# A graph layer whose first part becomes a pipeline over three batches, with two weight rows per frequency instead of three

## The chip, the cores and the metric

The kernel runs on one core of a Trainium2 chip. The metric is the device time of one launch in microseconds (us). TensorE does the matrix products (PE in the profile, PEld for its weight loads), VectorE (DVE) and ScalarE (ACT) the elementwise work, GpSimd (POOL) a little arithmetic, and SyncE (SP) issues most transfers. Data lie in HBM, in the on-chip SBUF (128 partitions) and in PSUM (eight banks, where TensorE writes).

## The reference, cut to what matters

```python
def ref(x, adj, ...):                      # x (32, 512, 256), adj (32, 512, 512), fp32
    h = max(layernorm(x), 0)
    c = relu(bn1(conv1(h)))                # kernel of width 1, 256 -> 256 channels
    x_conv = relu(bn2(conv2(c)) + h)       # kernel of width 17, 256 -> 256, padding 8
    s = h @ w_se.T + b_se                  # 3 features per node
    A = exp(-dist(s, s)) * adj
    x_nmp = A @ relu(h @ w_msg.T + b_msg)
    gi = concat(x_conv, x_nmp) @ w_ih.T + b_ih
    gh = h @ w_hh.T + b_hh
    r, z = sigmoid(gi_r + gh_r), sigmoid(gi_z + gh_z)
    n = tanh(gi_n + r * gh_n)
    return x + (1 - z) * n + z * h
```

The convolution of width 17 is done in the frequency domain. Each sequence of 512 is cut into 8 windows of 64, each window is transformed at 80 points, so there are 40 units: unit 0 holds the two real frequencies, units 1 to 39 a complex frequency each. In each unit a complex product over 256 input channels is needed, and it is done with three real products instead of four.

## The kernel before, in words

The 32 batches are worked in two groups of 16. The program has five stages, one after the other on TensorE:

1. First part of group 0. For each batch: layer norm (`layer_norm`, L221: four statistics and four aggregates on VectorE, one power on GpSimd at L229, four normalisations at L232), eight transposes to channels-by-nodes (L243) that VectorE evicts with the ReLU (L244), a store of that tile to HBM (`hd`, L245), the convolution of width 1 (L256, VectorE adds the shift at L259, ScalarE the ReLU at L260), and the transform of the windows (L270, ScalarE copies at L273 into `xf`). Beside it the 17 taps of conv2 are transformed (`weights_to_freq`, L197): `load_taps` brings 8 input channels of each of four quarters (two transfers per quarter, of 16 taps and of the 17th), small products over 17 taps run four at a time on four row groups (L206), VectorE and ScalarE evict them by turns (L213, L215), and SyncE stores them to `wd` in HBM (L218). There are 64 such products of four, in 16 pieces, spread over the first 12 batches (`early = 12`).
2. Nodes of group 0 (messages L333, features, factors L353, distances L367, affinity, aggregation L381), with the 40 units of group 0 (`product`, L284) spread over the batches: `load_unit` loads the unit's three weight rows, GpSimd forms `both` = re + im (L294), TensorE does six matmuls (L299), ScalarE and VectorE evict `y` (L300, L304).
3. First part of group 1, without weights.
4. The rest of group 0: back transform (L411), gates (L421), output (L464 to L467), with the 40 units of group 1.
5. Nodes and rest of group 1.

The order within each engine is set by a scheduler that takes the instructions in program order as a priority and moves them where it expects an engine to be free. Tiles come from pools with a number of buffers: `x` has 2, `hT` 2, `wst` 6, `w2p` 2, `wt` 3, `both` 2. A load into a buffer waits for the last reader of the tile that had it. In stage 1 SyncE issues, in one queue: the loads of `x`, the stores `hd`, the tap loads and the stores `wd`.

For each frequency `wd` holds three rows, worked out by the transform of the taps: Wr, and two sums of Wr and Wi, so that the three products (re + im)·Wr, re·(second row) and im·(third row) give what the back transform needs; the sums are in the constants:

```python
    weights[:, 3::3], weights[:, 4::3], weights[:, 5::3] = cos, -sin - cos, cos - sin
```

Of the kernel before, what the change touches and what calls it, by code (L numbers as in the profile page):

```python
# [1 line left out]

# [12 lines left out]
P = 128  # L15
# [9 lines left out]
L = 80  # L25
UNITS = L // 2
ROWS = 3 * UNITS


def dft_constants(taps):  # L30
# [10 lines left out]
    weights = np.zeros((L, ROWS))  # L41
# [4 lines left out]
    back[3::3], back[4::3], back[5::3] = 2 * (cos - sin).T, -2 * sin.T, -2 * cos.T  # L46

    return [a.astype(np.float32) for a in (forward, weights[:taps][::-1], back / L)]
# [3 lines left out]
def gnn_layer(  # L52
# [38 lines left out]
    def load_x(b):  # L91
        X[b] = work.tile([P, NC, D], FP, tag="x", name=f"x_{b}", bufs=2)
        nc.sync.dma_start(X[b], x[b].rearrange("(c p) d -> p c d", p=P))


    load_x(0)
    ident = consts.tile([P, P], FP, name="ident")
# [12 lines left out]
    taps = consts.tile([P, ROWS], FP, name="taps")  # L110
    taps_dram = nc.inline_tensor(taps_np, name="dft_taps").ap()
    for q in range(4):
        nc.scalar.dma_start(taps[32 * q : 32 * q + 16, :], taps_dram[0:16, :])
        nc.scalar.dma_start(taps[32 * q + 16 : 32 * q + KT, :], taps_dram[16:KT, :])
    back = consts.tile([ROWS, L], FP, name="back")
    nc.scalar.dma_start(back, nc.inline_tensor(back_np, name="dft_back").ap())
# [25 lines left out]
    ones = consts.tile([P, P], FP, name="ones")  # L142
    nc.vector.memset(ones, 1.0)
    row1 = bank("row1")
    for i, v in enumerate((scale1, shift1)):
        for c in range(DC):
            diag = work.tile([P, P], FP, tag="diag", name=f"diag_{i}_{c}")
            nc.vector.tensor_scalar(diag, ident, v[:, c : c + 1], None, op0=ALU.mult)
            nc.tensor.matmul(row1[:, i * D + c * P : i * D + (c + 1) * P], ones, diag, start=True, stop=True)
# [11 lines left out]
    def load_weights():  # L161
        nc.scalar.dma_start(wmsg[:, :, :D], w_msgT.rearrange("(c p) o -> p c o", p=P))
        nc.scalar.dma_start(wmsg[:, :, D:], w_seT.rearrange("(c p) t -> p c t", p=P))
        nc.scalar.dma_start(bmsg[:, :D], b_msg.to_broadcast([P, D]))
        nc.scalar.dma_start(bmsg[:, D:], b_se.rearrange("t o -> o t").to_broadcast([P, NS]))
        nc.scalar.dma_start(whh, w_hhT.rearrange("(c p) o -> p c o", p=P))
        nc.scalar.dma_start(wih, w_ihT.rearrange("(c p) o -> p c o", p=P))
# [10 lines left out]
    WD = dram.tile([ROWS, D, D], FP, name="wd")  # L178
# [8 lines left out]
    W2P, WST = {}, {}  # L187

    def load_taps(gen, pc):
        t = W2P[pc] = gen.tile([P, PI, D], FP, tag="w2p", name=f"w2p_{pc}", bufs=2)  # L190
        for q in range(4):
            i0 = QI * q + PI * pc
            src = w2T[i0 : i0 + PI].rearrange("i k o -> k i o")
            nc.sync.dma_start(t[32 * q : 32 * q + 16], src[0:16])
            nc.sync.dma_start(t[32 * q + 16 : 32 * q + KT], src[16:KT])

    def weights_to_freq(gen, pc, part):  # L197
        per = N // D
        for q in range(4):
            WST[q] = gen.tile([ROWS, SI, D], FP, tag="wst", name=f"wst_{pc}_{part}_{q}", bufs=6)  # L200
        for s in range(0, SI, per):
            i = part * SI + s
            ps = []
            for q in range(4):
                p = bank(f"pw_{pc}_{i}_{q}")
                nc.tensor.matmul(p[:ROWS, :], taps[32 * q : 32 * q + KT, :],  # L206
                                 W2P[pc][32 * q : 32 * q + KT, i : i + per, :], start=True, stop=True)
                ps.append(p)
            for q in range(4):
                dst = WST[q][:, s : s + per, :]  # L210
                src = ps[q][:ROWS, :].rearrange("r (i d) -> r i d", d=D)
                if q % 2:
                    nc.vector.tensor_copy(dst, src)  # L213
                else:
                    nc.scalar.copy(dst, src)  # L215
        for q in range(4):
            i0 = QI * q + PI * pc + SI * part
            nc.sync.dma_start(WD[:, i0 : i0 + SI, :], WST[q])  # L218


    def layer_norm(b):  # L221
# [5 lines left out]
        rstd = work.tile([P, NC], FP, tag="rstd", name=f"rstd_{b}")  # L227
        nc.vector.tensor_scalar(rstd, mv[:, :, 1], LN_EPS, None, op0=ALU.add)
        nc.gpsimd.tensor_tensor(rstd, rstd, minus_half[:, :NC], op=ALU.pow)  # L229
        XN[b] = X[b]  # L230
# [48 lines left out]
    def load_unit(pw, g, u):  # L279
        t = WT[g, u] = pw.tile([P, DC, 3, D], FP, tag="wt", name=f"wt_{g}_{u}", bufs=3)  # L280
        for ic in range(DC):
            nc.sync.dma_start(t[:, ic], WD[3 * u : 3 * u + 3, ic * P : (ic + 1) * P, :].rearrange("k p o -> p k o"))

    def product(pw, g, u, xf):  # L284
        load_unit(pw, g, u)
        wt = WT.pop((g, u))
        re, im = xf[:, :, 2 * u, :], xf[:, :, 2 * u + 1, :]
# [193 lines left out]
    def first_part(g, xf, between):  # L481
        b0, b1 = g * GB, (g + 1) * GB
        if b0 not in X:
            load_x(b0)
# [3 lines left out]
        for b in range(b0, b1):  # L488
            if b + 1 < b1:
                layer_norm(b + 1)  # L490
# [159 lines left out]
```

## Time and profile before

| | |
|---|---|
| median of 3 runs | 2166.65 us (2163.05 to 2168.56) |
| the profiled execution's own time | 2165.15 us |
| its span, first to last instruction | 2163.3 us |
| mean granted TensorE clock | 0.972 |
| TensorE busy, share of the span | 96% |
| VectorE, ScalarE, GpSimd busy | 41%, 26%, 5% |
| moved by transfers | 308.89 MB |

Busy time of TensorE is the union of modelled matmul spans, so a stretch that reads 95% can still hold waits. A wait is best read in the lists of waits and in the chain, which is the work followed back from the last instruction: each piece stands with its start and the time it added. In tables by stretches the columns are: start:end and length, busy us (and count) of each engine, the granted TensorE clock, the busy share of the transfer engines, and GB/s. Group rows end with: count | busy us in total, mean ns of one | idle us of the engine just before them and what ended it. Rows that begin with SPq show how long SyncE's queue needed to issue a transfer, which includes the time that it was held up.

### The profile page before, as it was taken

To read this page: it belongs to the slowest core of one execution; us is meant where nothing else is said; L and a number is where in the kernel's file an instruction comes from. 1 tells how busy PE (TensorE), PEld (TensorE's weight loads), DVE (VectorE), ACT (ScalarE), POOL (GpSimd) and SP (SyncE) were. 2 spreads that over 40 slices of the span, in tenths; PEclk is the share of its full clock that TensorE was granted. 3 is DMA by queue.
4 is the path that set the end of the run, shared out by engine and by line. 5 is a ranking of instruction groups with operands and counts; after the bars stand their busy time and mean duration, and the time that the engine had idled before them with its cause. 6 is when DMAs were issued, how large, how long until landed. Compare 5 with 4: busy or idle time off the path is not lost.

```text
span 2163.3 us, 20486 instructions
## 1 busy us (share of the span) xinstructions
PE 2074.0 (96%) x7616; PEld 1258.4 (58%) x7616; DVE 887.8 (41%) x1893; ACT 557.5 (26%) x882; POOL 97.4 (5%) x119
## 2 busy tenths in 40 slices
PE   5878999999998999999999999999999999999998
PEld 3655766666687555555565555555555555555554
DVE  5555655545586222322232223433334444333343
ACT  1333423333234111111111111222223222222231
POOL 1000010001011000000000000000000000000000
PEclk7787999999999999999999999999999999999999
DMA  7777789889945444464345436232232333322210
GB/s 211 233 246 246 226 232 245 247 237 239 286 143 170 132 146 137 143 187 147 123 149 182 139 116 145 71 70 67 67 67 67 77 84 86 89 67 67 67 39 20
DMA packets 257922, 308.89 MB, mean 143 GB/s; under 512 B 12831, under 2 KB 224799, under 8 KB 257823
## 3 DMA queue, kind: packets, MB, share of 16 engines
q1 hardware_dynamic: 243840, 272.93, 45.8%
q10 hardware_dynamic: 13983, 34.65, 4.3%
q8 instruction: 60, 0.98, 0.2%
q14 instruction: 39, 0.32, 0.1%
HBM read 202.68 MB, written 104.86 MB: 142 GB/s over the span
## 4 chain that ended last, share of the span: by engine, by line
PE 86%; DVE 7%; DMA 3%; issue 2%; ACT 1%; POOL 1%; SPq 0%; ACTq 0%; DVEq 0%; POOLq 0%
PE pg L421 30%; PE pn L381 10%; PE pgi L421 10%; PE py L299 8%; PE pc L411 5%; PE pgh L421 5%; PE pc L256 4%; PE pm L333 4%; PE px L270 2%; DMA x<-in_x_dram 2%; PE pw L206 2%; PE pd L367 1%; PE po L464 1%; DVE at L372 1%; DVE stats L225 1%
## 5 line engine op out<-in xcount | busy, mean ns | idle before, releaser
L421 PE MATMUL pg<-nmp,wih 128*128 128x512 f32 x512 | 240.8, 592 | 0.0
L421 PE MATMUL pg<-hT,whh 128*128 128x512 f32 x512 | 240.6, 592 | 0.0
L421 PE MATMUL pg<-xconv,wih 128*128 128x512 f32 x512 | 240.6, 592 | 0.0
L436 ACT ACTIVATE rz<-pg,brz 128x512 f32<-128x512 f32 x128 | 87.9, 687 | 558.3 <-PE pg L421 558.3
L381 PE MATMUL pn<-A,msg 128*128 128x512 f32 x512 | 227.2, 597 | 1.5 <-DVE A L373 1.5
L447 DVE SCALAR_TENSOR_TENSOR n<-pgh,vec,rz 128x512 f32<-128x512 f32 x64 | 47.8, 747 | 399.9 <-PE pgh L421 399.9
L304 DVE COPY y<-py 128x256 f32<-128x256 f32 x78 | 32.9, 423 | 395.9 <-PE py L299 395.9
L421 PEld LDWEIGHTS pg<-xconv,wih 128*128 128x128 f32 x512 | 97.3, 190 | 122.5 <-issue 122.5
L421 PEld LDWEIGHTS pg<-nmp,wih 128*128 128x128 f32 x512 | 97.2, 190 | 122.0 <-issue 121.7
L381 PEld LDWEIGHTS pn<-A,msg 128*128 128x128 f32 x512 | 98.0, 192 | 119.6 <-issue 114.4
L421 PEld LDWEIGHTS pg<-hT,whh 128*128 128x128 f32 x512 | 97.3, 191 | 108.3 <-issue 104.3
L299 PE MATMUL py<-wt,xf 128*128 128x256 f32 x640 | 153.2, 381 | 0.0
L372 DVE STREAM_TRANSPOSE at<-adj 128x512 f32<-128x512 f32 x128 | 134.4, 1084 | 13.5 <-DMA adj<-in_adj_dram 13.3
L256 PE MATMUL pc<-w,hT 128*128 128x256 f32 x512 | 134.5, 422 | 0.4 <-DVE hT L244 0.4
L333 PE MATMUL pm<-wmsg,hT 128*128 128x259 f32 x512 | 131.9, 412 | 0.0
L411 PEld LDWEIGHTS pc<-back,yt 120*128 120x128 f32 x1024 | 120.6, 193 | 18.4 <-issue 18.2
L449 ACT ACTIVATE n<-n,vec 128x512 f32<-128x512 f32 x64 | 46.2, 722 | 330.2 <-DVE n L448 330.2
L299 PEld LDWEIGHTS py<-wt,xf 128*128 128x128 f32 x640 | 121.6, 191 | 16.4
L333 PEld LDWEIGHTS pm<-wmsg,hT 128*128 128x128 f32 x512 | 123.3, 327 | 13.0 <-issue 6.8
L256 PEld LDWEIGHTS pc<-w,hT 128*128 128x128 f32 x512 | 107.5, 215 | 30.7 <-ACT wst L215 10.3
L411 PE MATMUL pc<-back,yt 120*128 120x80 f32 (+1 forms) x1024 | 119.2, 275 | 3.2 <-DMA yt<-yd 3.2
L421 PE MATMUL pgh<-hT,whh 128*128 128x512 f32 x256 | 121.9, 598 | 0.0
(82 smaller groups left out, 2312.3 us busy)
## 6 DMA issues: line engine op xcount, KB each, us to landing
wt<-wd SPq DMA_DIRECT2D x160, 384.0 KB
x<-in_x_dram SPq DMA_DIRECT2D x64, 512.0 KB
adj<-in_adj_dram SPq DMA_DIRECT2D x128, 256.0 KB
wd<-wst SPq DMA_DIRECT2D x64, 480.0 KB
yd<-y ACTq DMA_DIRECT2D x80, 384.0 KB
yt<-yd SPq DMA_DIRECT2D x64, 480.0 KB
hT<-hd SPq DMA_DIRECT2D x48, 512.0 KB
hd<-hT SPq DMA_DIRECT2D x32, 512.0 KB
```

Of the source, the lines that this page charges most:

```text
L206: nc.tensor.matmul(p[:ROWS, :], taps[32 * q : 32 * q + KT, :], W2P[pc][32 * q : 32 * q + KT, i : i + per, :], start=True, stop=True)
L256: nc.tensor.matmul(p[:, j, :], HT[b][:, ic, c * P : (c + 1) * P], w1[:, ic, :], start=(ic == 0), stop=(ic == DC - 1))
L270: nc.tensor.matmul(p[:, j * 2 * L : (j + 1) * 2 * L], H1[b][:, c0 + j, ic * P : (ic + 1) * P], fwd, start=True, stop=True)
L299: nc.tensor.matmul(dst, v[:, ic, :], wt[:, ic, k, :], start=(ic == 0), stop=(ic == DC - 1))
L333: nc.tensor.matmul(p[:, : D + NS], chunk(HT[b][:, ic, :], c), wmsg[:, ic, :], start=(ic == 0), stop=(ic == DC - 1))
L372: nc.vector.transpose(at.rearrange("p (j k) -> p j k", k=32), ADJ[b].rearrange("p j (q c) -> p c j q", c=NC)[:, mc])
L381: nc.tensor.matmul(p, MSG[b][:, mc, dc * P : (dc + 1) * P], A[b][:, mc, :], start=(mc == 0), stop=(mc == NC - 1))
L411: nc.tensor.matmul(p[:, t0:t1], YT[b][w][:, oc * P : (oc + 1) * P], back[:, u0 : u0 + t1 - t0], start=(w == 0), stop=(w == W - 1), skip_gr ...
L421: nc.tensor.matmul(p, w, v, start=(i == 0), stop=(i == len(terms) - 1))
L436: nc.scalar.activation(RZ[b][:, g, :], p, AF.Sigmoid, bias=brz[:, g : g + 1], scale=1.0)
L447: nc.vector.scalar_tensor_tensor(n, ph, b_hn[:, i : i + 1], RZ[b][:, i, :], op0=ALU.add, op1=ALU.mult)
L449: nc.scalar.activation(n, n, AF.Tanh, bias=b_in[:, i : i + 1], scale=1.0)
```

## The change

It has three parts.

The rows. `wd` holds Wr and Wi only (`WROWS` = 80 instead of 120), so a store of `wst` has 320 KB instead of 480 KB and `load_unit` loads 256 KB per unit in two transfers instead of 384 KB. `product` lets GpSimd form three tiles per unit: re + im, im − re (128x256 each), and `wsum` = Wr + Wi (128x512, new). The products are (im − re)·Wr, (re + im)·Wi and re·wsum, in this order; `wsum` is thus read last. The back transform's constants are adapted. The number and shape of the matmuls stay.

The first part, in both groups. `layer_norm` is split into `statistics` and `normalise`. In a step for batch b, three batches are in work: statistics and normalisation of b + 2, transposes of b + 1, convolution of b, and transform of the windows of b − 1. `x` gets 3 buffers, `wst` 8, and its loads from batch b0 + 3 on, as well as the tap loads after the first two, are issued by GpSimd's queue instead of SyncE's. The weight products are spread over all 16 batches, two products of four per batch, one before and one behind the windows; of eight evictions VectorE does three (before four). The block stands under `tc.manual_schedule()`, which keeps the program's order on each engine. `wih` and the other weights of the later stages are loaded at batch 8 by SyncE (before: at the start, by ScalarE's queue).

In the stage of the nodes two units, not one, stand before `factors` of the next batch. The taps' constants are laid out for four quarters and come in one transfer, not eight.

```diff
-    weights[:, 3::3], weights[:, 4::3], weights[:, 5::3] = cos, -sin - cos, cos - sin
+    weights[:, 2::2], weights[:, 3::2] = cos, -sin
...
-    def load_x(b):
-        X[b] = work.tile([P, NC, D], FP, tag="x", name=f"x_{b}", bufs=2)
-        nc.sync.dma_start(X[b], x[b].rearrange("(c p) d -> p c d", p=P))
+    def load_x(b, queue=nc.sync):
+        X[b] = work.tile([P, NC, D], FP, tag="x", name=f"x_{b}", bufs=3)
+        queue.dma_start(X[b], x[b].rearrange("(c p) d -> p c d", p=P))
...
-    WD = dram.tile([ROWS, D, D], FP, name="wd")
+    WD = dram.tile([WROWS, D, D], FP, name="wd")
...
-    def load_taps(gen, pc):
+    def load_taps(gen, pc, queue=nc.gpsimd):
...
+            queue.dma_start(t[32 * q : 32 * q + 16], src[0:16])
+            queue.dma_start(t[32 * q + 16 : 32 * q + KT], src[16:KT])
...
-                if q % 2:
-                    nc.vector.tensor_copy(dst, src)
+            if q == 3 or (q == 1 and s == 0):
+                nc.vector.tensor_copy(dst, src)
...
     def load_unit(pw, g, u):
-        t = WT[g, u] = pw.tile([P, DC, 3, D], FP, tag="wt", name=f"wt_{g}_{u}", bufs=3)
-        for ic in range(DC):
-            nc.sync.dma_start(t[:, ic], WD[3 * u : 3 * u + 3, ic * P : (ic + 1) * P, :].rearrange("k p o -> p k o"))
+        t = WT[g, u] = pw.tile([P, 2, DC, D], FP, tag="wt", name=f"wt_{g}_{u}", bufs=3)
+        for k in range(2):
+            nc.sync.dma_start(t[:, k], WD[2 * u + k].rearrange("(i p) o -> p i o", p=P))
...
-            both = pw.tile([P, DC, P], FP, tag="both", name=f"both_{g}_{u}", bufs=2)
-            nc.gpsimd.tensor_tensor(both, re, im, op=ALU.add)
+            both = pw.tile([P, 2, DC, P], FP, tag="both", name=f"both_{g}_{u}", bufs=2)
+            nc.gpsimd.tensor_tensor(both[:, 0], re, im, op=ALU.add)
+            nc.gpsimd.tensor_tensor(both[:, 1], im, re, op=ALU.subtract)
+            wsum = pw.tile([P, DC, D], FP, tag="wsum", name=f"wsum_{g}_{u}", bufs=2)
+            nc.gpsimd.tensor_tensor(wsum, wr, wi, op=ALU.add)
             p2 = bank(f"py2_{g}_{u}")
-            terms = [(p[:, :D], both), (p[:, D : 2 * D], re), (p2[:, :D], im)]
+            terms = [(p2[:, :D], both[:, 1], wr), (p[:, D : 2 * D], both[:, 0], wi), (p[:, :D], re, wsum)]
...
         for b in range(b0, b1):
-            if b + 1 < b1:
-                layer_norm(b + 1)
-            if b + 2 < b1:
-                load_x(b + 2)
-            between(b - b0)
-            conv1(b)
+            one, two = between(b - b0)
+            if b + 3 < b1:
+                load_x(b + 3, nc.gpsimd)
+            if b + 2 < b1:
+                statistics(b + 2)
             if b + 1 < b1:
                 transpose_h(b + 1)
-            windows_to_freq(b, xf)
+            if b + 2 < b1:
+                normalise(b + 2)
+            conv1(b)
+            for step in one:
+                step()
+            if b > b0:
+                windows_to_freq(b - 1, xf)
+            for step in two:
+                step()
+        windows_to_freq(b1 - 1, xf)
...
-                    for u in mine[:1]:
+                    for u in mine[:2]:
                         product(pw, 0, u, xf)
                     if more:
                         factors(b + 1)
-                    for u in mine[1:2]:
-                        product(pw, 0, u, xf)
                     aggregate(b)
```

Three places show how instructions move. The first is TensorE in the first part of group 0. `pc` is the convolution, `phT` a transpose, `px` the transform of the windows, `pw` a weight product. Before, at batch 2 (h_2 goes into px in the step in which it is made):

```order
L256 MATMUL pc_2_0_549<-w_77,hT_420 128x256 x4
L256 MATMUL pc_2_2_556<-w_77,hT_420 128x256 x4
L243 MATMUL phT_0_564<-ident,x_362 128x128 x4
L243 MATMUL phT_1_570<-ident,x_362 128x128 x4
L270 MATMUL px_0_0_577<-fwd,h_2_548 128x160 x2
L270 MATMUL px_0_2_581<-fwd,h_2_548 128x160 x2
L270 MATMUL px_1_0_585<-fwd,h_2_548 128x160 x2
L270 MATMUL px_1_2_589<-fwd,h_2_548 128x160 x2
L206 MATMUL pw_0_0_616<-w2p_396,taps 120x512
L206 MATMUL pw_0_1_618<-w2p_396,taps 120x512
```

Now, the step of batch 2:

```order
L257 MATMUL phT_0_467<-ident,x_266 128x128 x4
L257 MATMUL phT_1_473<-ident,x_266 128x128 x4
L270 MATMUL pc_2_0_485<-w_79,hT_361 128x256 x4
L270 MATMUL pc_2_2_492<-w_79,hT_361 128x256 x4
L213 MATMUL pw_0_0_503<-w2p_204,taps 80x512
L213 MATMUL pw_0_1_505<-w2p_204,taps 80x512
L213 MATMUL pw_0_2_507<-w2p_204,taps 80x512
L213 MATMUL pw_0_3_509<-w2p_204,taps 80x512
L284 MATMUL px_0_0_515<-fwd,h_1_379 128x160 x2
L284 MATMUL px_0_2_519<-fwd,h_1_379 128x160 x2
L284 MATMUL px_1_0_523<-fwd,h_1_379 128x160 x2
L284 MATMUL px_1_2_527<-fwd,h_1_379 128x160 x2
```

The transposes (of batch 3) went ahead of the convolution of batch 2, four weight products stand between, and the windows transformed are those of batch 1, made a step earlier.

The second place is GpSimd's queue in the first part of group 0. `rstd` is the power of the layer norm, in the order of the batches. Before, the powers stand alone:

```order
L229 TENSOR_TENSOR rstd_226<-rstd_226,minus_half 128x4
L229 TENSOR_TENSOR rstd_259<-rstd_259,minus_half 128x4
L229 TENSOR_TENSOR rstd_355<-rstd_355,minus_half 128x4
L229 TENSOR_TENSOR rstd_460<-rstd_460,minus_half 128x4
L229 TENSOR_TENSOR rstd_603<-rstd_603,minus_half 128x4
```

Now, from the power of batch 2 on (the pair of tap loads stands four times):

```order
L240 TENSOR_TENSOR rstd_278<-rstd_278,minus_half 128x4
L99 DMA x_346<-in_x_dram 128x4x256
L240 TENSOR_TENSOR rstd_358<-rstd_358,minus_half 128x4
L200 DMA w2p_442<-in_w2T_dram 16x8x256
L201 DMA w2p_442<-in_w2T_dram 1x8x256
...
L99 DMA x_451<-in_x_dram 128x4x256
L240 TENSOR_TENSOR rstd_463<-rstd_463,minus_half 128x4
L99 DMA x_547<-in_x_dram 128x4x256
```

Between the power of batch 3 (`rstd_358`) and that of batch 4 (`rstd_463`) stand now eight tap loads, which wait for the last product that reads the old `w2p`, and a load of `x`. That is so at every second batch, six times in all.

The third place is TensorE in the nodes of group 0, around `factors` (psl and psr). `py` is a unit, `pn` the aggregation. Before:

```order
L299 MATMUL py_5_2203<-wt_5_2199,both_5_2204 128x256 x2
L299 MATMUL py_5_2203<-wt_5_2199,xf_215 128x256 x2
L299 MATMUL py_0_5_2206<-wt_5_2199,xf_215 128x256 x2
L353 MATMUL psl_2216<-ident,fl 128x128 x4
L353 MATMUL psr_2223<-ident,fr 128x128 x4
L299 MATMUL py_6_2234<-wt_6_2230,both_6_2235 128x256 x2
L299 MATMUL py_6_2234<-wt_6_2230,xf_215 128x256 x2
L299 MATMUL py_0_6_2237<-wt_6_2230,xf_215 128x256 x2
L381 MATMUL pn_0_2248<-A_2134,msg_2026 128x512 x4
```

Now:

```order
L317 MATMUL py_0_5_2224<-wt_5_2214,both_5_2219 128x256 x2
L317 MATMUL py_5_2218<-wt_5_2214,both_5_2219 128x256 x2
L317 MATMUL py_5_2218<-wsum_5_2222,xf_213 128x256 x2
L317 MATMUL py_0_6_2244<-wt_6_2234,both_6_2239 128x256 x2
L317 MATMUL py_6_2238<-wt_6_2234,both_6_2239 128x256 x2
L317 MATMUL py_6_2238<-wsum_6_2242,xf_213 128x256 x2
L371 MATMUL psl_2254<-ident,fl 128x128 x4
L371 MATMUL psr_2261<-ident,fr 128x128 x4
L399 MATMUL pn_0_2269<-A_2149,msg_2032 128x512 x4
```

`psl` and `psr` moved behind the second unit, and the last pair of each unit now reads `wsum`.

More of the change, by code (lines that the diff above doesn't have):

```diff
@@ L193, in load_taps, with weights_to_freq @@
             src = w2T[i0 : i0 + PI].rearrange("i k o -> k i o")
-            nc.sync.dma_start(t[32 * q : 32 * q + 16], src[0:16])
-            nc.sync.dma_start(t[32 * q + 16 : 32 * q + KT], src[16:KT])
-    def weights_to_freq(gen, pc, part):
+            queue.dma_start(t[32 * q : 32 * q + 16], src[0:16])
+            queue.dma_start(t[32 * q + 16 : 32 * q + KT], src[16:KT])
+    def weights_to_freq(gen, pc, i):
         per = N // D
-        for q in range(4):
[L200 to L203, printed above, removed]
-            for q in range(4):
[L205 to L211, printed above, removed]
-                if q % 2:
[L213 to L218, printed above, removed]
```

119 lines of the change are left out of this document (75 added, 44 removed).

## The prediction

> **What bounds the kernel now.** I read the page first, then a table by the program's stages, the chain of waits in the first part, and a timeline of one stretch there.
>
> ```profile
> span 2163.3 us, 20486 instructions
> PE 2074.0 (96%) x7616; PEld 1258.4 (58%) x7616; DVE 887.8 (41%) x1893; ACT 557.5 (26%) x882; POOL 97.4 (5%) x119
> PE 86%; DVE 7%; DMA 3%; issue 2%; ACT 1%; POOL 1%; SPq 0%; ACTq 0%; DVEq 0%; POOLq 0%
> ```
>
> TensorE holds 86% of the chain, so most of the program can't gain from anything but fewer or faster matmuls, and the change has just as many of the same shape. The question is where the other 14% lie. By stage (first part, nodes, first part of group 1, rest, last stage):
>
> ```profile
> 0.00:251.50 251.50, 200.69 (x905) 145.23 (x906) 138.32 (x359) 81.64 (x160) 18.22 (x25) 0.81 0.74 232
> 251.50:583.60 332.10, 317.67 (x1247) 218.11 (x1247) 181.22 (x432) 103.77 (x169) 34.71 (x41) 0.99 0.88 245
> 583.60:703.50 119.90, 108.84 (x641) 96.86 (x639) 84.64 (x247) 46.17 (x96) 15.50 (x16) 1.00 0.51 172
> 703.50:1395.00 691.50, 686.67 (x2314) 389.19 (x2315) 184.09 (x287) 121.23 (x178) 28.92 (x37) 0.99 0.48 140
> 1395.00:2163.30 768.30, 760.11 (x2516) 409.05 (x2514) 299.54 (x568) 204.69 (x279) 0.00 (x0) 1.00 0.28 67
> ```
>
> The first part is the only stage with large holes: TensorE is idle for 51 of 251.5 us, and its granted clock is 0.81. What its work would take without holes is read from the chain, where pieces stand back to back at full clock:
>
> ```profile
> 222.81 3.45 PE pc L256 x16
> 226.27 0.89 PE phT L243 x8
> 227.17 4.30 DMA x<-in_x_dram
> 242.10 0.55 PE px L270 x4
> 242.67 1.90 PE px L270 x12
> 251.56 2.90 PE pm L333 x12
> ```
>
> A batch needs 3.45 + 0.89 + 0.55 + 1.90 = 6.8 us, and the transposes of one batch are followed by 4.30 us of waiting for the `x` of a later one. The weight products and the engines around them, in a stretch of 25 us:
>
> ```profile
> 139.45 1.99 PE L206 MATMUL pw<-w2p,taps 17*120 17x512 f32 x16
> 140.62 1.62 SPq L245 DMA_DIRECT2D hd<-hT  x1
> 142.34 1.63 SPq L93 DMA_DIRECT2D x<-in_x_dram  x1
> 143.47 0.69 DVE L259 TENSOR_TENSOR h<-pc,shift_row 128x512 f32<-128x512 f32 x1 [1.28 <-PE pc L256]
> 144.06 7.74 SPq L218 DMA_DIRECT2D wd<-wst  x4
> 145.74 0.74 DVE L225 BATCH_NORM_STATS2 stats<-x 128x6 f32<-128x256 f32 x2
> 147.52 0.17 DVE L228 TENSOR_SCALAR rstd<-mv 128x4 f32<-128x4 f32 x1
> 147.83 1.01 POOL L229 TENSOR_TENSOR rstd<-rstd,minus_half 128x4 f32<-128x4 f32 x1 [22.42 <-DVE rstd L228]
> 148.87 1.38 DVE L232 TENSOR_SCALAR x<-x,mv,rstd 128x256 f32<-128x256 f32 x4 [1.19 <-POOL rstd L229]
> 150.17 1.28 DVE L213 COPY wst<-pw 120x512 f32<-120x512 f32 x2
> 151.37 1.28 DVE L244 TENSOR_SCALAR hT<-phT 128x512 f32<-128x512 f32 x2
> 154.00 0.44 SPq L194 DMA_DIRECT2D w2p<-in_w2T_dram  x1
> 154.48 0.63 SPq L195 DMA_DIRECT2D w2p<-in_w2T_dram  x1
> 161.16 3.25 PE L206 MATMUL pw<-w2p,taps 17*120 17x512 f32 x8 [3.05 <-DVE wst L213]
> ```
>
> Two things alternate here. VectorE runs a whole layer norm with a wait of 1.19 us for GpSimd in it, and evictions that TensorE needs stand behind it (the 3.05 us at 161.16). And SyncE's queue is held up by its transfers: four stores of 480 KB take 7.74 us, 1.94 each. No engine is full; a chain through all of them repeats for each batch.
>
> **First part of group 0.** TensorE's step is now 6.8 + 1.99 = 8.8 us (16 weight products of the profile per batch). VectorE's: statistics from 145.74 to 147.69, 1.95; transposes' eviction 1.28; normalisation 1.38; two additions 1.28; three copies 1.92: 7.8 us. The power (0.14 to start, 1.01) runs beside the eviction of the transposes, so its wait goes if GpSimd is free. The eviction that ends a step is also the one ahead of the next statistics, so VectorE trails TensorE by one copy (0.64), and the banks that the second four weight products need come free that much later: 8.8 + 0.7 = 9.5 us for the chain. Transfers per step: four stores of 320 KB at 1.94·2/3 = 1.29, `hd` 1.62, `x` 1.63, and half a set of taps, 2·(0.44 + 0.63) = 2.14: 10.6 us if the queues' times add up, less where two queues overlap. The price of a transfer that GpSimd issues stands in no row. From below, SyncE's 0.44 and 0.63; from above, the 1.01 us that GpSimd spends on a power of four elements, for each transfer. At every second batch eight tap loads and an `x` stand ahead of a power; they can start when TensorE ends the last product, and VectorE needs the power 0.6 + 1.95 + 1.28 = 3.8 us later. GpSimd needs 4·1.07 + 0.44 + 1.01 = 5.7 us by the lower price and 10·1.01 = 10.1 by the upper, so VectorE, and the additions and banks behind it, are held 1.9 to 6.3 us, six times. I take the middle, 4 us: 24 us, or 1.6 per step. With the 9.5 that is 11.1; the transfers, with 2.6 MB of weights at batch 8 (`wih`, `whh` and `wmsg` by their shapes; some 9 us by the 245 GB/s above, 0.6 per step), come to 11.2. As neither wholly hides in the other, I take 11.5.
>
> The start: VectorE evicts the first transposes as before, then statistics, power and normalisation of batch 1.
>
> ```profile
> 13.01 1.28 DVE L244 TENSOR_SCALAR hT<-phT 128x512 f32<-128x512 f32 x2
> 27.34 6.53 PE L256 MATMUL pc<-w,hT 128*128 128x256 f32 x16
> ```
>
> 13.0 + 1.3 + 1.95 + 1.2 + 1.4 = 18.9, transposes 1.5 (an estimate, at the low clock), the convolution 6.5, the products 2 to 3: step 1 begins near 30 us, where before the first convolution ended only at 33.9. Then 30 + 15·11.5 + 2.5 for the last windows = 205 us against 251.5: **−46**. The range of this term: at 9.5 per step 175 (−76); if every transfer that GpSimd issues paces the step, below, −10.
>
> A rule speaks against the transfers on GpSimd's queue. The Trainium skill (SBUF — State Buffer, sections "SBUF: two separate sides" and "Who interferes with whom") states that GpSimd can't write the descriptors of a transfer while VectorE runs an operation in a mode that takes both ports, and that the normalisation's kind (tensor_scalar) can run in one. By that rule each `x` load could wait out a normalisation of 1.38 us; the sum would then go towards the second rival. The rows are against it:
>
> ```profile
> L232 DVE TENSOR_SCALAR x<-x,mv,rstd 128x256 f32<-128x256 f32 x128 | 44.8, 411 | 22.8 <-POOL rstd L229 22.8
> L336 DVE TENSOR_TENSOR msg<-pm,bmsg 128x256 f32<-128x256 f32 x128 | 52.4, 416 | 0.0
> ```
>
> The normalisation takes 411 ns for 256 elements, as long as an addition that reads PSUM, so nothing shows it in a doubled mode.
>
> **Nodes.** Here the waits list has one wait of TensorE that matters:
>
> ```profile
> PE psl L353 <- DVE fr L347: 13.2, 13, 2.1
> 270.14 2.59 PE py L299 x12
> 272.74 6.88 PE pn L381 x16
> ```
>
> `psl` waits for the features, 13.2 us in all. With a second unit (2.59 us) ahead of it none of the 13 waits, 2.1 at most, outlasts it; `psl` only has to be done before `pd`, behind 6.88 us of `pn`. I take −11 of 13.2. The smaller loads (256 for 384 KB) gain nothing more: no wait of TensorE for `wt` is in the list.
>
> What is added is GpSimd's work.
>
> ```profile
> L294 POOL TENSOR_TENSOR both<-xf 128x256 f32<-128x256 f32 x78 | 63.0, 809 | 832.5 <-PE py L299 803.0 <-ACT xf L273 29.4
> ```
>
> Per unit 0.81 becomes 2·0.81 + 1.62 (`wsum` has twice the elements) = 3.2 us. A unit comes every 332/40 = 8.3 us here. Its two sums start when the unit two before has read its own, so for the second of a pair there are at least a unit and `pn`, 2.59 + 6.88 = 9.5 us. The cover is 6 us: I cost it at nothing. `wsum` also needs `wt` to have landed some 2 us earlier; three buffers of `wt` stay.
>
> **First part of group 1 and the rest.**
>
> ```profile
> PE px L270 <- ACT h L260: 6.9, 10, 1.7
> PE pc L411 <- DMA yt<-yd: 3.2, 1, 3.2
> ```
>
> 119.9 us for 16·6.8 = 109 us of work: the windows no longer follow the convolution at once, so their waits (6.9) go; but the step now begins with transposes of batches 16 and 17 in a row, and between them stand eviction, statistics, power and normalisation (1.28 + 1.95 + 1.15 + 1.38 = 5.8 us) with nothing for TensorE. −2. The `yt` loads still wait behind the last `hT` buffers, with 2.5 us more of windows ahead: −2. In the rest GpSimd's longer work meets VectorE's:
>
> ```profile
> 700.00:1390.00 690.00, 27.43 (x32) 0.99 0.48 141
> 1400.00:2163.00 763.00, 22.14 (x32) 1.00 0.28 68
> ```
>
> These are the rows of the last addition of the output (L454): 857 ns each where GpSimd forms `both`, 692 where it is idle. The output's transposes follow it at once. Bounds: 0 to 16·1.62 = 26 us, if each batch meets a whole `wsum`; I take +2, since a unit's sums now start only behind its predecessor's second product, when that addition is mostly past.
>
> **The sum**: −46 − 11 − 2 − 2 + 2 = −59; 2163.3 − 59 = 2104 of span, 1.85 us around it as before, and the profiled execution lay 1.5 under the median: **2107 us**.
>
> **The rivals.**
> 1. *The pipeline runs at the chain's 9.5 us*: GpSimd's transfers are cheap and overlap SyncE's. For it: in stage 2 the engines moved 245 GB/s at a share of 0.88, where stage 1 had 0.74. −76, nodes −13, others −6: 2070. Chance 0.20.
> 2. *GpSimd's transfers pace the first part*: each `x` (512 rows of 1 KB) or set of taps takes long to issue, and the powers wait at every batch. At 14 us per step the stage takes 30 + 210 + 2.5 = 242: −9; with −13 elsewhere 2144. Chance 0.14; the Trainium skill's rule above is one way to it.
> 3. *GpSimd and VectorE shut each other out in the rest*: the upper bound, +24 more: 2131. Chance 0.07. The Trainium skill (SBUF — State Buffer, "Who interferes with whom") says so: a VectorE instruction with two SBUF inputs and a GpSimd instruction that reads SBUF exclude each other, for the whole instruction. The 857 against 692 ns agree that they meet.
> 4. *TensorE waits for `wsum`* (slower): if the chain of slot, three GpSimd operations and VectorE's exclusions makes each unit late by its own 1.62 us, 78 units cost 126 us: 2107 + 126 = 2233. It decides from 59/78 = 0.76 us per unit on. Against it: the 6 us of cover. Chance 0.07.
> 5. *The gain of the first part returns as waits* behind `wd`, which is now finished at the last batch and not at the twelfth: no change. Chance 0.02.
>
> **How the numbers follow.** The forecast has 0.50. The range 2070 to 2148 takes in the first three rivals and leaves out the fourth, and what lies beyond the first. About 0.3% (6.5 us) is what a measurement of this kernel can tell from no change. Faster: 0.50 + 0.20 + 0.14 + 0.07 = 0.91; same 0.02; slower 0.07.
>
> **What would show it.** Right: the nodes begin near 205 us; steps of about 11.5 us with a longer one at every second batch, where VectorE's normalisation waits for a power behind tap loads; `psl` gone from the waits; `py` waiting for nothing. Wrong: even steps (rival 1 or 2), transposes of the output waiting in the rest (3), or TensorE waiting for `wsum` (4).

## The result, and the profile after

The changed kernel takes 2096.19 us (median of 4 runs, 2095.26 to 2100.15) against 2167.56 (4 runs): a ratio of 0.9678, with a 95% interval of 0.9659 to 0.9697. The forecast was 2107, within 2070 to 2148. The profiled execution has a span of 2094.7 us, 68.6 less than before. By the same five stages (columns as before):

```profile
0.00:200.10 200.10, 172.34 (x905) 122.03 (x905) 133.60 (x354) 80.96 (x176) 55.36 (x87) 0.91 0.75 236
200.10:521.80 321.70, 313.97 (x1248) 218.81 (x1247) 204.99 (x409) 102.05 (x169) 108.02 (x118) 0.98 0.80 223
521.80:637.80 116.00, 107.37 (x642) 99.21 (x639) 94.45 (x259) 41.63 (x97) 28.91 (x33) 0.97 0.53 176
637.80:1326.30 688.50, 684.07 (x2314) 388.54 (x2315) 176.47 (x287) 121.23 (x178) 101.26 (x112) 0.99 0.41 127
1326.30:2094.70 768.40, 760.10 (x2516) 409.04 (x2514) 299.76 (x568) 204.87 (x279) 0.00 (x0) 1.00 0.27 67
```

| term of the sum | predicted | by these stages |
|---|---|---|
| first part of group 0 | −46 | −51.4 |
| nodes | −11 | −10.4 |
| first part of group 1, and the `yt` wait | −2, −2 | −3.6, −0.3 |
| rest | +2 | −3.0 |
| last stage | 0 | +0.1 |
| sum | −59 | −68.6 |

**First part.** The transposes that begin the first and the last full step show the mean step: (180.82 − 27.31)/13 = 11.8 us, where 11.5 was predicted.

```profile
27.31 1.09 PE L257 MATMUL phT<-ident,x 128*128 128x128 f32 x8
...
180.82 1.09 PE L257 MATMUL phT<-ident,x 128*128 128x128 f32 x8
```

Steps alternate, 13.2 to 13.6 us with tap loads and about 10.3 without. One pair, as stretches:

```profile
84.30:97.90 13.60, 11.31 (x61) 7.66 (x57) 8.06 (x20) 5.48 (x12) 6.87 (x11) 0.85 0.76 254
97.90:108.20 10.30, 10.30 (x58) 7.71 (x57) 7.92 (x20) 4.56 (x11) 1.03 (x1) 0.86 0.61 178
```

Both have a granted clock of 0.85 or 0.86, and in the short one TensorE is never idle. The timeline of the long one:

```profile
84.76 0.58 POOL L200 DMA_DIRECT2D w2p<-in_w2T_dram  x1 [6.46 <-PE pw L213]
...
88.72 0.53 POOL L201 DMA_DIRECT2D w2p<-in_w2T_dram  x1
...
89.28 0.80 POOL L99 DMA_DIRECT2D x<-in_x_dram  x1
...
89.79 1.35 PE L284 MATMUL px<-fwd,h 128*128 128x160 f32 x8
90.09 1.03 POOL L240 TENSOR_TENSOR rstd<-rstd,minus_half 128x4 f32<-128x4 f32 x1
91.16 1.62 DVE L246 TENSOR_SCALAR x<-x,mv,rstd 128x256 f32<-128x256 f32 x4 [2.44 <-POOL rstd L240]
...
92.70 1.28 DVE L273 TENSOR_TENSOR h<-pc,shift_row 128x512 f32<-128x512 f32 x2
...
93.43 2.05 PE L284 MATMUL px<-fwd,h 128*128 128x160 f32 x8 [2.29 <-DVE h L273]
...
95.41 2.55 PE L213 MATMUL pw<-w2p,taps 17*80 17x512 f32 x8
```

This is the predicted hold: eight tap loads and an `x` ahead of the power, VectorE waiting 2.44 us in the normalisation, the additions behind it, and TensorE waiting 2.29 us for them. What the sum did not have is the last row: eight products that take 1.10 us elsewhere take 2.55. (The profile has two rows for each of these matmuls, 256 in all, so eight rows are one product of four, and the program has 32 of these; the 64 named ahead of the prediction count rows.) The granted clock in short stretches (columns: TensorE busy, clock, transfer share, GB/s):

```profile
90.00:92.00 2.00, 1.15 (x8) 1.00 1.01 334
92.00:93.40 1.40, 0.00 (x0) 1.00 0.86 312
93.40:95.40 2.00, 1.97 (x8) 0.63 0.95 342
95.40:97.90 2.50, 2.50 (x10) 0.50 0.49 195
97.90:100.00 2.10, 2.10 (x10) 0.50 0.55 152
100.00:102.00 2.00, 2.00 (x9) 0.81 0.96 260
102.00:104.00 2.00, 2.00 (x13) 1.00 1.01 272
```

Behind a wait of 2.29 us the clock is at half for some 6 us; the four stretches below 1.00 lose 0.74 + 1.25 + 1.05 + 0.38 = 3.4 us, more than the wait. The six waits of TensorE are 1.87 to 2.70 us long, and behind each the clock falls to 0.50. The Trainium skill (TensorE: Matmul & The Clock Gate, "Why this matters for your kernels") puts the drop to half at idle gaps over about 3 us; here 1.87 us were enough, and an experiment below has longer waits without a drop.

The price of a transfer that GpSimd issues, for which the prediction had only bounds, as groups:

```profile
L99 POOL DMA_DIRECT2D x<-in_x_dram x26 | 20.7, 798 | 3.1 <-DMA w2p<-in_w2T_dram 1.4 <-PE pc L270 1.1 <-PE px L284 0.4
L200 POOL DMA_DIRECT2D w2p<-in_w2T_dram x24 | 13.2, 549 | 37.5 <-PE pw L213 37.5
L201 POOL DMA_DIRECT2D w2p<-in_w2T_dram x24 | 12.7, 529 | 0.2 <-issue 0.2
```

**Nodes.** The waits list of TensorE in this stage:

```profile
PE psl L371 <- DVE fr L365: 5.2, 2, 3.3
```

The groups of VectorE there, those that make the features:

```profile
L364 DVE TENSOR_SCALAR fr<-st 128x48 f32<-128x48 f32 x16 | 18.0, 1124 | 0.0
...
L360 DVE TENSOR_TENSOR st<-st 128x12 f32<-128x12 f32 x16 | 7.7, 478 | 0.0
```

And the row of before that stands against L364:

```profile
L346 DVE TENSOR_SCALAR fr<-st 128x48 f32<-128x48 f32 x16 | 2.9, 184 | 0.0
```

The wait for `psl` fell from 13.2 to 5.2 us although an instruction that makes the features became six times as long. The timeline shows what it meets:

```profile
281.59 1.30 POOL L312 TENSOR_TENSOR wsum<-wt 128x512 f32<-128x512 f32 x1
...
281.68 1.26 DVE L364 TENSOR_SCALAR fr<-st 128x48 f32<-128x48 f32 x1
...
283.36 0.60 PE L371 MATMUL psl<-ident,fl 128*128 128x128 f32 x4
```

VectorE's instruction ends with GpSimd's `wsum`, and here `psl` doesn't wait for it, since a unit is still on TensorE.

**Rest.** The output's last addition (L472, in the kernel before L454) took 857 ns before in this stage and 692 in the last. Now:

```profile
640.00:1320.00 680.00, 21.99 (x32) 0.99 0.41 126
1330.00:2094.00 764.00, 22.13 (x32) 1.00 0.27 67
```

687 ns in both: GpSimd's work no longer meets it. And `yt` is still waited for, by the waits list:

```profile
PE pc L429 <- DMA yt<-yd: 2.9, 1, 2.9
```

Its loads in SyncE's queue (SPq) wait for the windows that the pipeline moved to the end, 3.1 us in two waits, where before it was 2.0 in one:

```profile
SPq L417 <- PE px L284: 3.1, 2, 1.8
```

### The profile page after: what moved, and what is told of

It reads as the page before. It is cut to its first block, busy times and chain, and to the rows that moved or that the text cites. A ratio compares the mean times of both kernels' runs of the same rounds, so it can differ in the third digit from the quotient of the medians.

```text
span 2094.7 us, 20904 instructions
## 1 busy us (share of the span) xinstructions
PE 2037.9 (97%) x7616; PEld 1237.6 (59%) x7616; DVE 909.3 (43%) x1877; ACT 550.7 (26%) x898; POOL 293.6 (14%) x349
## 4 chain that ended last, share of the span: by engine, by line
PE 87%; DVE 1%; DMA 1%; issue 0%; ACT 0%; SPq 0%; POOL 0%; DVEq 0%; ACTq 0%
PE pg L439 31%; PE pgi L439 10%; PE pn L399 10%; PE py L317 9%; PE pm L351 5%; PE pc L429 5%; PE pgh L439 5%; PE pc L270 3%; PE pd L385 2%; PE px L284 1%; PE po L482 1%; PE phT L257 1%; PE psr L371 1%; PE psl L371 1%; DMA adj<-in_adj_dram 0%; DVE at L390 0%
## 5 line engine op out<-in xcount | busy, mean ns | idle before, releaser
L454 ACT ACTIVATE rz<-pg,brz 128x512 f32<-128x512 f32 x128 | 87.9, 687 | 541.4 <-PE pg L439 527.0
L317 PE MATMUL py<-wt,both 128*128 128x256 f32 x624 | 148.1, 380 | 0.0
L309 POOL TENSOR_TENSOR both<-xf 128x256 f32<-128x256 f32 x78 | 60.0, 769 | 617.8 <-PE py L317 576.0
L390 DVE STREAM_TRANSPOSE at<-adj 128x512 f32<-128x512 f32 x128 | 134.4, 1085 | 10.4 <-DMA adj<-in_adj_dram 10.1
L317 PEld LDWEIGHTS py<-wt,both 128*128 128x128 f32 x624 | 116.8, 190 | 24.6 <-issue 11.3
L270 PE MATMUL pc<-w,hT 128*128 128x256 f32 x512 | 121.7, 393 | 0.0
```

What stands on the lines that cost most here:

```text
L270: nc.tensor.matmul(p[:, j, :], HT[b][:, ic, c * P : (c + 1) * P], w1[:, ic, :], start=(ic == 0), stop=(ic == DC - 1))
L309: nc.gpsimd.tensor_tensor(both[:, 0], re, im, op=ALU.add)
L317: nc.tensor.matmul(dst, v[:, ic, :], w[:, ic, :], start=(ic == 0), stop=(ic == DC - 1))
L390: nc.vector.transpose(at.rearrange("p (j k) -> p j k", k=32), ADJ[b].rearrange("p j (q c) -> p c j q", c=NC)[:, mc])
L454: nc.scalar.activation(RZ[b][:, g, :], p, AF.Sigmoid, bias=brz[:, g : g + 1], scale=1.0)
```

## Experiments: which part brings what

The theory at this point was the prediction's: the order of the first part brings most, less what the power's place in GpSimd's queue costs, and the order of the nodes the rest. The rivals: the shorter stores and loads bring it, or the transfers pace the first part. Each ratio below is against the kernel before, measured on the same chip; its medians there lie between 2165.0 and 2167.1 us. The lines are those of one profiled execution.

**The order of the nodes alone**, on the kernel before.

```diff
-                    for u in mine[:1]:
+                    for u in mine[:2]:
                         product(pw, 0, u, xf)
                     if more:
                         factors(b + 1)
-                    for u in mine[1:2]:
-                        product(pw, 0, u, xf)
```

> The kernel before with one edit: the second unit of each batch ahead of the factors. By the prediction's term for the nodes, which is this edit alone: 13.2 us of waits of psl go, 11 of them gained: 2155, within 4. If the gain of the nodes came from the smaller loads instead: no change, 2163 to 2170.

2151.67 us (ratio 0.9925, 0.9903 to 0.9948), some 15 us gained; the waits for `psl` in the nodes:

```profile
PE psl L353 <- DVE fr L347: 1.2, 1, 1.2
```

The term was right in its cause, and this edit alone is worth more than 11: the stage takes 318 us, before 332.

**The rows alone**, on the kernel before: 80 rows in `wd`, loads of two rows, three GpSimd operations.

```diff
-    WD = dram.tile([ROWS, D, D], FP, name="wd")
+    WD = dram.tile([WROWS, D, D], FP, name="wd")
...
-            nc.gpsimd.tensor_tensor(both, re, im, op=ALU.add)
+            nc.gpsimd.tensor_tensor(both[:, 0], re, im, op=ALU.add)
+            nc.gpsimd.tensor_tensor(both[:, 1], im, re, op=ALU.subtract)
+            nc.gpsimd.tensor_tensor(wsum, wr, wi, op=ALU.add)
```

> The kernel before with only the two rows per frequency: 320 KB stores, 256 KB loads, and GpSimd's two sums and wsum; first part, scheduler and order of the nodes as before. Theory (the order of the first part carries its gain): the first part stays near 250 us, since VectorE still runs a whole layer norm ahead of the evictions; the time is 2160, within 6 of it. Rival (the transfers carried it): 16 pieces of 4 stores get 0.65 us shorter each, 42 us of SyncE's queue, and the first part ends 25 to 42 us earlier: 2125 to 2142. If TensorE waits for wsum, the nodes and the rest grow and the time lies above 2170.

2186.7 us (1.0091, 1.0075 to 1.0108): slower than before. The first part ends at 244, 7 us earlier, where the rival had 25 to 42; and the nodes take 355 and not 332. The waits list of the nodes names the cause, and it isn't a wait for `wsum`:

```profile
PE psl L362 <- DVE fr L356: 34.2, 16, 2.2
```

**Rows and order**, both edits above together.

> The kernel before with the two rows per frequency and with the second unit ahead of the factors; first part as before. The rows alone took 2187, with 34 us of waits of psl. Theory (GpSimd's wsum makes the features late, and the second unit ahead of psl covers that): psl waits under 8 us, and the time is 2150 to 2160. Rival (the cover only works with the pipeline of the first part): psl still waits 20 us or more, 2172 to 2187.

2145.58 us (0.9905, 0.9879 to 0.9932). The same two rows that cost some 20 us alone cost nothing behind the other order. The wait in the nodes:

```profile
PE psl L362 <- DVE fr L356: 3.9, 4, 1.2
```

From here to the changed kernel (0.9678) only the first part differs, in both groups: 0.0227 of 2167 us, 49 us, for the pipeline with its buffers and queues, where −46 was predicted for group 0 and −4 for group 1 and `yt`.

**The old order in the changed kernel**: the first diff backwards.

> The changed kernel with the second unit of a batch put back behind the factors, as before. Theory (a second unit ahead of psl hides the features): the waits of psl come back, 5.2 us in 2 waits to 13 us or more in a dozen, and with GpSimd's longer work beside the features, which take longer now, rather more: the time is 2104 to 2116. Rival (the nodes gained by the smaller loads or otherwise): the time is within 4 of 2096.

2141.7 us (0.9878, 0.9858 to 0.9897): some 45 us lost, far beyond my expectation. I had priced the old wait of `psl`, and the longer features with no more than the words "rather more":

```profile
PE psl L371 <- DVE fr L365: 36.1, 15, 3.7
```

These waits say something on the clock too. Thirteen of the 15 are 2.23 or 2.24 us long. Behind ten of them the granted clock stays at 1.00, behind three it falls to 0.50 for some 3 us; and it stays at 1.00 behind one of 3.73 us. The stretches behind two waits of 2.23 and 2.24 us, at 308.88 and at 352.42:

```profile
308.80:312.20 3.40, 3.32 (x20) 3.06 (x21) 0.78 (x3) 1.57 (x2) 0.38 (x1) 1.00 1.15 232
352.40:355.80 3.40, 3.38 (x14) 2.95 (x15) 0.54 (x2) 1.66 (x2) 0.00 (x0) 0.59 1.15 232
```

So the length of a wait doesn't decide alone whether the clock falls.

**The old order, and `wsum` on VectorE**:

```diff
-            nc.gpsimd.tensor_tensor(wsum, wr, wi, op=ALU.add)
+            nc.vector.tensor_tensor(wsum, wr, wi, op=ALU.add)
```

> The changed kernel with the second unit behind the factors as before, and wsum formed by VectorE and not by GpSimd; the two sums of the spectra stay with GpSimd. With the old order alone the time was 2142, and psl waited 36 us for the features. Theory (wsum on GpSimd holds VectorE's feature instructions, 193 ns become 1050 to 1120): the constants of the features are back near 200 ns, psl waits some 13 us as before the change, and the time is 2112 to 2125, with 0.7 us of VectorE per unit added beside the rest. Rival (psl waits longer since the units or their loads come later): the features stay at 1000 ns or psl still waits over 30 us, and the time is 2135 or above.

2120.03 us (0.9795, 0.9762 to 0.9828). VectorE's groups in the nodes:

```profile
L360 DVE TENSOR_TENSOR st<-st 128x12 f32<-128x12 f32 x16 | 7.0, 437 | 0.0
...
L364 DVE TENSOR_SCALAR fr<-st 128x48 f32<-128x48 f32 x16 | 2.8, 177 | 0.0
```

And the wait of TensorE:

```profile
PE psl L371 <- DVE fr L365: 18.8, 15, 3.3
```

Half of the waiting goes with `wsum` (13 us were expected to be left), and the constants are as short as before, so it was GpSimd's `wsum` that held the features. The squares of L360 are still long; the two sums of the spectra remain on GpSimd.

**`wsum` twice** on GpSimd, in the changed kernel.

```diff
             nc.gpsimd.tensor_tensor(wsum, wr, wi, op=ALU.add)
+            nc.gpsimd.tensor_tensor(wsum, wr, wi, op=ALU.add)
```

> The changed kernel with wsum formed twice, one after the other, on GpSimd: 1.29 us more per unit. By the prediction's cover of 6 us per unit for TensorE: nothing, 2092 to 2100. If TensorE waits for wsum (rival 4), 78 units by 1.29 us: up to 2196. If what counts is how long GpSimd holds VectorE, the features of each of 16 batches come up to 1.3 us later, against what cover the second unit still gives: 2096 to 2117, with psl waiting in more than its 2 places.

2111.63 us (0.9744, 0.9714 to 0.9774), 15 us more, and no wait of TensorE for `wsum` in the list; in the nodes `psl` waits again:

```profile
PE psl L372 <- DVE fr L366: 12.4, 8, 3.3
```

The cover of 6 us that the prediction counted is there for the products; for the features it is less than 1.3 us.

**The pipeline with three rows**: the changed kernel with 120 rows in `wd`, the old loads and one GpSimd sum.

> The changed kernel with three rows per frequency as before (480 KB stores, 384 KB loads, one sum on GpSimd), pipeline and order of the nodes as changed. Theory (the step is a chain of TensorE, VectorE and the power, and the stores are hidden): steps stay at 11.8 us on average, the first part ends near 200 us, and the time is 2094 to 2102. Rival (the transfers pace the step): 4 stores at 1.94 us, hd and x at 0.4 to 1.6 each and the taps make 11 to 13 us of SyncE's queue per step; steps of 13 us or more, the first part ends near 230, and the time is 2120 to 2130. In the nodes, without wsum, the constants of the features (193 ns before, 1124 after) should be back near 193 ns if it is GpSimd's longer work that slows them.

2119.45 us (0.9784, 0.9760 to 0.9808). The first part ends at 216 and not at 200, so the two rows are worth 16 us there: between the theory (nothing) and the rival (30). But not by the queue time that I had added up, 7.74 us for four stores of 480 KB. By the timeline four take less than half of that here:

```profile
105.44 3.57 SPq L226 DMA_DIRECT2D wd<-wst  x4
```

The power comes later instead: the normalisation waits for it up to 6.0 us. Ahead of it in GpSimd's queue the load of `x` is held, by the profile behind tap loads, for 9.5 us in six waits, against 1.4 in three with two rows; why the larger stores hold it is not shown. The nodes take 326 us, some 4 more than in the changed kernel, and one of their units waits 3.2 us for its weights. In the nodes, without `wsum`, the group of the features' constants is short:

```profile
L360 DVE TENSOR_SCALAR fr<-st 128x48 f32<-128x48 f32 x16 | 3.1, 191 | 0.0
```

## Experiments: what is left in the first part

**The taps behind the power**: same loads, same queue.

```diff
-            load_taps(gen, pc + 2)
+            LATER.append(pc + 2)
...
                 statistics(b + 2)
+            while LATER:
+                load_taps(pools["gen"], LATER.pop(0))
```

> The changed kernel with the eight tap loads queued on GpSimd behind the next power and not ahead of it; same loads, same queue. Theory (the normalisation waits for the power behind tap loads): the six waits of 3.0 us go, and the long steps of 13.4 us become as short as the others. If the lower granted clock (0.86 against 1.00) comes from those stalls, the short steps shrink from 10.3 to 9.5 or 9.8 too: the first part ends near 170 to 175 and the time is 2066 to 2071. If the clock stays, all steps are 10.3 and the time is 2077. Rival (the transfers pace the step, and the stall only takes the place of another wait): the mean step stays within 0.3 of 11.8 and the time within 5 of 2096.

2084.72 us (0.9616, 0.9598 to 0.9635), more than the 2066 to 2077 expected; its profiled execution, the fastest of the four (2078.6), ends the first part at 183. Two steps of the middle, one with taps and one without, then a late one:

```profile
87.40:97.40 10.00, 9.72 (x58) 6.84 (x56) 7.91 (x20) 5.19 (x13) 2.60 (x3) 1.00 0.92 259
97.40:107.00 9.60, 9.44 (x57) 6.65 (x56) 7.83 (x20) 4.60 (x11) 5.36 (x9) 1.00 0.89 273
...
149.00:164.00 15.00, 11.45 (x57) 8.24 (x57) 10.32 (x33) 5.15 (x13) 2.25 (x2) 0.89 0.67 224
```

In these steps no normalisation waits for a power, the clock is 1.00, and steps without a wait take 9.8 us on average: the low clock followed the waits. The end is worse than expected: step 117 to 129 has 12 us, and 149 to 164 has 15.

**The weights of the gates later**: as above, and

```diff
-                first_part(1, xf, lambda i: ([], []))
+                first_part(1, xf, lambda i: load_gates(i - 2) if i >= 2 else ([], []))
```

where `load_gates` loads a part of `wih`, then `back`, then a part of `whh`, one per batch.

> The changed kernel with the tap loads behind the power, and with the loads of wih, back and whh (all but the message weights) moved from the first part to the first part of group 1, one per batch. With the taps behind the power alone the time was 2085, and steps were 9.6 to 10.0 us up to 117 us into the run, and 11.7, 10.4 and 15.1 where the weights landed. Theory (with the stalls gone the transfer engines are full, at shares of 0.93 to 1.05, and 2.4 MB of weights cost their own time): the first part ends near 172 to 175 and not at 183, and the time is 2072 to 2079. Rival (the long steps come from the last batches themselves, or group 1 gives the time back): 2082 to 2090.

2077.3 us (0.9599, 0.9569 to 0.9628; its runs, 2076 to 2083, overlap those of the kernel above). The steps from 117 us on now have 9.6 to 10.4 us, so the weights had made those long. The late step stays, and the first part still ends at 182:

```profile
148.00:164.00 16.00, 13.11 (x56) 9.29 (x55) 10.74 (x34) 5.26 (x12) 2.26 (x2) 0.69 0.57 178
```

My theory fails for it. In that step VectorE waits 3.48 us for an `x` and then takes the statistics of two batches, of the last one and of batch 16, which the scheduler of the next stage has placed there. The same lies in the changed kernel's step at 169.3.

**The taps on SyncE**, at the place that GpSimd's loads had.

```diff
-            load_taps(gen, pc + 2)
+            load_taps(gen, pc + 2, nc.sync)
```

> The changed kernel with the tap loads issued by SyncE at the same places in the program as GpSimd issues them now; the loads of x stay with GpSimd. Theory (what costs is that the power stands behind tap loads in GpSimd's queue): the waits of the normalisation go as with the taps behind the power, the granted clock of the first part rises from 0.89 towards 1.00, and the time is 2079 to 2090. Rival (SyncE's queue has no room for eight more transfers, 4.3 us at 0.53 each, every second step, and hd and wd behind them free their buffers late): steps of 11.8 us or more, and the time is 2094 or above.

2085.99 us (0.9623, 0.9585 to 0.9660; the profiled execution, 2074.4, is the fastest of four): like the taps behind the power, so what cost was the power's place and not GpSimd's queue as such. The scheduler leaves batch 16's statistics out of the first part in this build, and no step is over 10.4 us. TensorE is done with the first part at 176 us, and then:

```profile
PE pm L351 <- DMA hT<-hd: 7.6, 1, 7.6
```

**Both of these, and then the first tile of the nodes from GpSimd's queue**: two candidates, the second with

```diff
-        nc.sync.dma_start(HT[b], HD[b])
+        queue = nc.gpsimd if b == 0 and "nodes" in pools and "rest" not in pools else nc.sync
+        queue.dma_start(HT[b], HD[b])
```

> A candidate: the changed kernel with the tap loads on SyncE's queue, and wih, back and whh loaded during the first part of group 1. With the taps on SyncE alone the time was 2086, TensorE ended the first part at 176 us and then waited 7.6 us for the first tile of the nodes, behind stores and weights. Theory (the transfers are what is left): 2.4 MB less, 9 us at some 270 GB/s, take most of that wait away: 2068 to 2079. Rival (the nodes wait for the stores of the last weights all the same): 2080 to 2088.

> The last candidate: taps on SyncE, gate weights later, and the first tile of the nodes loaded by GpSimd's queue instead of SyncE's. Without that last edit TensorE waited 7.5 us for this tile at the start of the nodes, and the time was 2080. Theory (the tile is late because its load stands in SyncE's queue behind eight stores that wait for the last evictions): the wait falls under 2 us and the time is 2070 to 2077. Rival (the transfer engines are full then, whoever issues, or the next wait, for the first adj, takes its place): 2078 to 2083.

The first: 2080.29 us (0.9594, 0.9569 to 0.9619), with the wait for the tile still 7.5 us; 2.4 MB fewer transfers didn't bring it earlier, so the theory of full transfer engines falls for this wait. The second: 2073.95 us (0.9578, 0.9561 to 0.9594; runs 2072.31 to 2075.84), and the wait is gone: the load had stood in SyncE's queue behind eight stores that wait for the last evictions. This is the lowest time; what it gains over the first lies between 3.5 us by the ratios, whose intervals overlap, and 6 by the medians. Its first part:

```profile
27.00:170.00 143.00, 139.83 (x804) 98.35 (x803) 110.69 (x273) 73.42 (x162) 22.31 (x25) 0.99 0.89 259
```

## Why the prediction was right, step by step

- **The first part** (−46; −51 by the stages, 49 between two kernels that differ in it alone). The mechanism was as described, and the start and step lay close (27.3 for 30, 11.8 for 11.5). I had priced the last two steps like the others, though they have no layer norm left: from the last full step's transposes the stage takes 19.3 us, where the sum has 25.5. That and the earlier start outweigh the longer steps. Inside the step two sizes were off and made up for each other. The hold by the power was sized at 4 us, the middle of 1.9 to 6.3. With the prices measured it is 4·(0.549 + 0.529) + 0.80 + 1.03 − 3.8 = 2.3, near the lower end, and the six waits are 2.2 to 3.0 us, 14.8 together. But such a wait takes clock with it (3.4 us in the one shown; all six long steps have a mean clock of 0.84 to 0.87), which the prediction did not have. The chain without the hold was sized at 9.5 and is 9.8. Two steps, a long and a short one, take 23.8 us on average, some 4 more than two at 9.8. I had taken just these 4 for the hold alone, so the step came out right by luck. The queue times that I summed to 11.2 us per step are no bound either: with the taps behind the power the same transfers fit into steps of 9.8 us on average. (The 2.6 MB of weights at 245 GB/s are 10.7 us and not the 9 in the sum, which is 0.1 per step.)
- **The nodes** (−11; −10.4). The cause, a second unit ahead of `psl`, is shown by that edit alone, which gains 15. The step that failed is beside it: "I cost it at nothing". I looked for the cover of GpSimd's 3.2 us where TensorE's products wait for them. It does not lie there. `wsum` holds VectorE, so the features come late, and the same second unit of which I took only the old wait had to cover that too. Without it the rows alone make the kernel before 20 us slower, and the changed kernel loses 45.
- **First part of group 1 and `yt`** (−2 and −2; −3.6 and −0.3). The hole at the start measures 5.7 us for the 5.8 worked out, and no wait of the windows (6.9) is left; these two make 1.2 of the 3.6, and the rest is not explained. The sum is right, the second part isn't: the `yt` loads wait longer for the last windows (3.1 us, before 2.0), which the pipeline put at the very end.
- **The rest** (+2; −3.0). The sign was wrong. With three rows in the otherwise changed kernel the addition takes 869 ns (26.07 us for 30), with two rows 687, and with the rows alone in the kernel before 687 too (18.55 us for 27). So it is with two rows that GpSimd's work no longer meets this addition, where I had expected it to meet it longer.
- **The rivals.** The transfers by GpSimd do not pace the step (second): each costs 0.53 to 0.80 us, and taking the taps off its queue or only behind the power gives the same time. Even steps at the chain's length (first) are what the kernels with the taps moved show, and 2074 is near that rival's 2070. That GpSimd holds VectorE (third) is true, but in the nodes and not in the rest. TensorE waiting for `wsum` (fourth) does not happen: a second `wsum` of 1.3 us per unit costs 15 us, not 100. No wait behind `wd` took the gain back (fifth); one of 7.6 us came up only where the taps went to SyncE and the first part ended earlier still.

What stays open: which edit of the first part carries the 49 us, since its order, the third buffer of `x`, the eight of `wst` and the loads of `x` on GpSimd's queue were only changed together; why the clock falls behind waits of 1.9 to 2.7 us in the first part and mostly not behind such waits in the nodes; and by which rule VectorE's `fr` is held. The Trainium skill (SBUF — State Buffer, "Who interferes with whom") names instructions with two SBUF inputs, which fits the squares of L360 (200 ns before, 478 after), and of those with one input only the two-port modes, in which `fr` would have to run; its own 184 ns don't show that.

## What to carry to other kernels

Look for the cover of added GpSimd work at VectorE's short instructions as well as at its consumer: here constants of 0.2 us became 1.1 us, and the wait for them was 34 us where one unit stood ahead of it and 4 us where two did. Put a short operation that others wait for ahead of the transfers in the same queue; that one move was worth 11 us here, and the load of the next stage's first tile in a queue with no stores ahead of it another 3.5 to 6. Look at the granted clock behind a wait of TensorE before pricing it by its length: here it cost up to 3.4 us more in the first part, and in the nodes mostly nothing.

## What the runs showed of the hardware that was not expected

- After TensorE had waited 2.29 us in the first part, the granted clock was 0.50 for some 6 us, which cost 3.4 us; behind waits of 1.87 us there it fell too. In the nodes, in the kernel with the old order, ten of thirteen waits of 2.23 or 2.24 us left it at 1.00, and so did one of 3.73.
- A VectorE instruction with one SBUF input that started 0.09 us after a GpSimd addition lasted as long as that (1.26 us beside 1.30), where it takes 184 ns alone.
- A transfer costs GpSimd 0.53 us for 8 KB from one tap as for 128 KB from sixteen (0.55), and 0.80 us for 512 KB of `x`.
- One store of 480 KB held SyncE's queue for 0.32 to 2.50 us in the kernel before (median 0.90) and for 0.32 to 3.00 in the pipeline with the same stores (median 0.55): the 1.94 that the prediction scaled is a state of the queue, not a price of the transfer.
